# Attention and mixture-of-experts block on one core: TensorE order as written, whole mixes, a later load addition

## The chip, the cores and the metric

The kernel runs on one core of a Trainium2 chip, in one launch. Times are device microseconds from the chip's own clock; the figure for a kernel is the median of several runs. A profile is one execution of the same program with the hardware profiler on. Engines are named as in the profile: PE is TensorE (with PEld, its weight loads), DVE is VectorE, ACT is ScalarE, POOL is GpSimd, SP issues DMAs.

## What is computed

The input x is 8 sequences of 512 rows of 256 floats (fp32). Four layers follow each other, each added to x after a layer norm of its input: a scan layer, a mixture of experts, attention, and the same mixture of experts again. Cut to what matters here:

```
x = x + scan(layernorm(x))
x = x + ffn(layernorm(x))
x = x + attn(layernorm(x))
x = x + ffn(layernorm(x))

attn(x):   # per sequence, 16 heads of 16
    q, k, v = x @ Wqkv.T
    s = clip(q k^T / 4, -10, 10), masked causally
    return softmax(s) v @ Wout.T

ffn(x):    # 4096 rows, 16 experts, 4 picked per row
    picks, gains = route(sigmoid(x @ router.T))
    routed = sum of gain * (silu(x g_e) * (x u_e)) d_e over the picks
    return routed + (silu(x sg) * (x su)) sd     # shared experts
```

## The kernel before

**Stages.** There are four, one after the other: a stretch for the scan layer with the routing and the shared experts of the first mixture; the routed experts of the first mixture; a stretch for attention with the routing and the shared experts of the second mixture; the routed experts of the second mixture, with the sums that make the output. Routed and shared results go to two DRAM arrays (`parts`), and the next stage loads both and adds them (`load_sum`, L135 to L142).

**Attention, batch by batch.** `Attention.main(b)` works on one sequence, as four groups of four heads (two values of `o`, two of `w`). Because of causality, the key tiles of a group are packed into three banks (`BANKS`): key tile 0 (512 columns), tiles 3 and 1 (128 + 384), tile 2 (256). For each bank, `weights` issues one block of score matmuls (L1026, 32x128 array tiles, four heads beside each other), two exponentials on ScalarE (L1037), and on VectorE a mask with a clamp (L1040) and, for the rest, a clamp (L1048). The scores have two PSUM pairs of banks (kind `pair`), so the next block needs both exponentials of the block before the last to be done. `mix` multiplies a bank's weights by v (L1061, 128x32 tiles) into one accumulator of the group, `po`. `share` copies `po` (ScalarE), transposes it (four transposes, L1077, `pto`), and VectorE divides by the row sum (`rec`, `o_a`, L1079 and L1080). After the four groups, `o` is transposed (`pt_oa`) and projected (L416, `py_a`).

**What else stands in a batch of the stretch.** `stretch` (the function that drives both stretches) puts beside each other, in batch b: attention of b; the sends of batch b − 2 (16 indirect DMAs that GpSimd issues, L647, each after slots and gain of its rows, L630 and L637); the projections q, k, v of b + 1 (L971, L989); the shared experts of b − 2 (`pg`, L892; `pd`, L920); the norm and the logits of b − 1 for the router (`sorted_m`, L400; transposes `pt_m` and copies `xT_m`, L364 and L366; logits `pl_m`, L540); the rest of the routing; and for batch b + 2 the load, its addition (L141) and its norm (`normed`: statistics on VectorE, L378 and L379, the power `rstd_l` on GpSimd, L397, then `xn` on VectorE, L400) and transposes. Transposes, logits, projections, shared experts and `po` share four PSUM banks of kind `one`.

**What sets the order.** Each piece is a generator whose steps yield a number of columns, and `beside` always takes the piece that has done the smallest share of its columns; `timed` places steps at given shares of a batch. That is the written order. The framework's scheduler may then move an instruction on its engine ahead of others that it does not depend on, by its own estimate of when inputs are ready; so the order that each engine runs is not the written one. `tc.keep_in_program_order(made)` pins one instruction: it stays behind the instruction of its engine that was written just before it. Nothing was pinned before. Engines run their own lists in order, and wait where an input is not there.

In the old attention steps, a bank of the last group's mix follows each score block of the next group:

```
for i in range(len(BANKS)):
    yield weights(o, w, i, at)
    if last is not None:
        yield mix(*last[0:2], i, last[2])
```

**Early batches.** `prepared(b)` loads, adds and norms batches 0 and 1 of the attention stretch during the routed experts of the first mixture, by GpSimd's queue. In these experts, per block: `up` copies of weights on VectorE (L786), matmuls with `gate` and `up` (L804), and the down projection (L832).

Of the kernel before, what the change touches and what calls it, by code (L numbers as in the profile page):

```python
# [15 lines left out]
P = 128  # L16
# [54 lines left out]
def tile_hybrid_block(  # L71
# [64 lines left out]
    def load_sum(i: int, b: int, more, queue=nc.sync):  # L136

        x_sb = xpool.tile([P, NT, D], FP, tag="x", name=f"x{i}_{b}")
        queue.dma_start(out=x_sb, in_=rows_of(parts[i][0], b))
        queue.dma_start(out=more, in_=rows_of(parts[i][1], b))  # L140
        nc.vector.tensor_add(x_sb, x_sb, more)  # L141
        x_tiles[b] = x_sb  # L142


# [151 lines left out]

    class Piece:
# [53 lines left out]
    def turned(src, tag: str, into, copies, home=None):  # L353

        rows = src()
        if home is None:
            dst = work.tile([P, KD, T], FP, tag="kb4", name=f"xT_{tag}", bufs=KB)
        else:
            dst = home(f"xT_{tag}")
        into(dst)  # L360
        for k in range(KD):
            pt = bank([P, NT, P], f"pt_{tag}_{k}")
            for t in range(NT):
                nc.tensor.transpose(pt[:, t, :], rows[:, t, k * P : (k + 1) * P], ident)  # L364
            flat = pt.rearrange("p t q -> p (t q)")
            copies[k](dst[:, k, :], flat)  # L366
            yield T // 2
# [40 lines left out]
    def add_projection(b: int, lhs_of, w_sb, n: int, tag: str):  # L408

        x_sb = x_tiles[b]  # L410
        for half in range(2):
            py = bank([P, 2, D], f"py_{tag}_{half}")
            for j in range(2):
                t = 2 * half + j
                for c in range(n):
                    nc.tensor.matmul(  # L416
                        py[:, j, :],
                        lhsT=lhs_of(c)[:, t * P : (t + 1) * P],
                        rhs=w_sb[:, c, :],
                        start=(c == 0),  # L420
                        stop=(c == n - 1),
                    )
                yield n * D
            rows = x_sb[:, 2 * half : 2 * half + 2, :]
            nc.vector.tensor_add(rows, py, rows)


    class Scan:
# [21 lines left out]
        def main(self, b: int, xnT):  # L450
            tag = f"s{b}"

            def steps():
                y_sb = []
                for c in range(NI):
                    pz = bank([P, T], f"pz_{tag}_{c}")
                    for k in range(KD):
                        nc.tensor.matmul(
                            pz,
# [3 lines left out]
                            stop=(k == KD - 1),  # L463
                        )
                    bias = b_in_sb[:, c : c + 1]
# [69 lines left out]
    def logits(i: int, b: int, tag: str, held):  # L535
        xnT = held["xnT"]
        pl = bank([P, NT, E], f"pl_{tag}")
        for t in range(NT):
            for k in range(KD):
                nc.tensor.matmul(  # L540
                    pl[:, t, :],
# [3 lines left out]
                    stop=(k == KD - 1),  # L545
                )
            yield
# [4 lines left out]
    def choices(i: int, b: int, tag: str, held):  # L552
# [52 lines left out]
        flat = sel.rearrange("p t e -> p (t e)")  # L605
        nc.tensor.matmul(pr[:, 0].rearrange("p t e -> p (t e)"), lhsT=tri, rhs=flat, start=True, stop=True)
        nc.tensor.matmul(pr[:, 1].rearrange("p t e -> p (t e)"), lhsT=ones, rhs=flat, start=True, stop=True)
        row = small.tile([P, NT + 1, E], FP, tag="row", name=f"row_{tag}", bufs=3)
# [52 lines left out]
    def blocks(i: int, table):  # L661
# [60 lines left out]
        for c in range(CAND):  # L722
            nc.tensor.matmul(
                pe, lhsT=cand_e.to_broadcast([P, P]), rhs=chosen[:, c, :], start=(c == 0), stop=(c == CAND - 1)
            )
        expert = small.tile([P, NBLK], FP, tag="expert", name=f"expert_{tag}", bufs=1)
        nc.scalar.copy(expert, pe)
        lines = work.tile([1, 2, NBLK], I32, tag="col", name=f"lines_{tag}", bufs=COLS)
        for which in range(2):
            pl = bank([1, NBLK], f"pl_{tag}_{which}")  # L730
            for c in range(CAND):
                nc.tensor.matmul(
                    pl, lhsT=cand_at[:, which, c : c + 1], rhs=chosen[:, c, :], start=(c == 0), stop=(c == CAND - 1)
                )
            if which == 0:
# [11 lines left out]
    def routed(i: int, table, beside):  # L747
# [41 lines left out]
        def turn(n: int):  # L789
            rows = held[n][2]  # L790
            pt = bank([P, KD, P], f"pt_{i}_{n}", "misc")
            for k in range(KD):
                nc.tensor.transpose(pt[:, k, :], rows[:, k * P : (k + 1) * P], ident)  # L793
            nc.scalar.copy(rows[:, ROW : ROW + D], pt.rearrange("p k q -> p (k q)"))  # L794

        def up(n: int):
# [4 lines left out]
            for s in range(2):  # L801
                for f in range(KF):
                    for k in range(KD):
                        nc.tensor.matmul(  # L804
                            ph[:, s, f * P : (f + 1) * P],
# [3 lines left out]
                            stop=(k == KD - 1),  # L809
                        )  # L810
            act = rows[:, ROW + D : ROW + D + F]
# [16 lines left out]
        def down(n: int):  # L828
            w, _, rows, act, gain = held.pop(n)
            py = bank([P, D], f"pyr_{i}_{n}", "y")  # L830
            for f in range(KF):
                nc.tensor.matmul(  # L832
                    py,
# [3 lines left out]
                    stop=(f == KF - 1),  # L837
                )

# [37 lines left out]
    def shared_experts(i: int, b: int, xnT_of, tanh: bool):  # L877
# [3 lines left out]
        def steps():  # L881
            xnT = xnT_of()
            acts = []
            for n in range(NSH):
# [3 lines left out]
                for f in range(KF):  # L888
                    pair = [bank([P, T], f"pg_{tag}_{n}_{f}_{which}") for which in range(2)]
                    for dst, w in zip(pair, (g_sb, u_sb)):  # L890
                        for k in range(KD):
                            nc.tensor.matmul(  # L892
                                dst,
# [3 lines left out]
                                stop=(k == KD - 1),  # L897
                            )
                        if dst is pair[0]:
# [14 lines left out]
            for half in range(2):  # L914
                py = bank([P, 2, D], f"pd_{tag}_{half}")
                for j in range(2):
                    t = 2 * half + j
                    for n in range(NSH):
                        for f in range(KF):
                            nc.tensor.matmul(  # L920
                                py[:, j, :],
# [3 lines left out]
                                stop=(n == NSH - 1 and f == KF - 1),  # L925
                            )
                    yield NSH * KF * D
# [17 lines left out]
    class Attention:  # L945
# [7 lines left out]
        def load(self, b: int):  # L953
            load_sum(0, b, kb4(f"more0_{b}"))

        def project(self, b: int, xnT):
# [8 lines left out]
            def steps():  # L965
                nc.gpsimd.memset(v_sb, 1.0)
                for o in range(NO):
                    for which in range(2):
                        pq = bank([P, T], f"pq_{tag}_{o}_{which}")
                        for k in range(KD):  # L970
                            nc.tensor.matmul(  # L971
                                pq,
# [3 lines left out]
                                stop=(k == KD - 1),  # L976
                            )
                        if which == 0:
# [5 lines left out]
                for h in range(2):  # L984
                    pv = bank([P, 2, D], f"pv_{tag}_{h}")
                    for j in range(2):
                        t = 2 * h + j
                        for k in range(KD):
                            nc.tensor.matmul(  # L989
                                pv[:, j, :],  # L990
# [3 lines left out]
                                stop=(k == KD - 1),  # L994
                            )
                        nc.scalar.copy(
# [7 lines left out]
        def main(self, b: int, made):  # L1004
# [4 lines left out]
            def weights(o: int, w: int, i: int, at):  # L1009
# [12 lines left out]
                for c in tiles:  # L1022
                    n = T - c * P
                    for j in range(HG):
                        r = slice(32 * j, 32 * j + 32)
                        nc.tensor.matmul(  # L1026
                            ps[j // 2][:, j % 2, col : col + n],
# [3 lines left out]
                            stop=True,  # L1031
                        )
                        at[c, j] = es[j // 2][:, j % 2, col : col + n]
                    col += n
                mixed = len(tiles) * P
                for two in range(2):
# [11 lines left out]
                    nc.vector.tensor_scalar(es[two][:, :, mixed:], es[two][:, :, mixed:], LOW, TOP, ALU.max, ALU.min)  # L1048
                return T + (len(tiles) - 1) * T

            order = [c for tiles, _ in BANKS for c in tiles]

            def mix(o: int, w: int, i: int, at):
# [4 lines left out]
                for c in BANKS[i][0]:  # L1058
                    for j in range(HG):
                        h = 8 * o + 2 * j + w  # L1060
                        nc.tensor.matmul(  # L1061
                            at["po"][32 * j : 32 * j + 32, c * P : T],
# [4 lines left out]
                            tile_position=(0, 32 * j),  # L1067
                        )
                return len(BANKS[i][0]) * T

            def share(o: int, w: int, at):
# [4 lines left out]
                for t in range(NT):  # L1076
                    nc.tensor.transpose(pt[:, t].rearrange("p j c -> p (j c)"), oT[:, t * P : (t + 1) * P], ident)  # L1077
                rec = small.tile([P, NT, HG], FP, tag="rec", name=f"rec_{tag}_{o}_{w}")
# [7 lines left out]
            def steps():  # L1086
                held["o"] = kb4(f"o_{tag}")
                groups = [(o, w, {}) for o in range(NO) for w in range(2)]
                last = None
                for o, w, at in groups:  # L1090
                    for i in range(len(BANKS)):
                        yield weights(o, w, i, at)
                        if last is not None:
                            yield mix(*last[0:2], i, last[2])
                    if last is not None:
                        share(*last)
                        yield T // 2
                    last = o, w, at
                for i in range(len(BANKS)):
                    yield mix(*last[0:2], i, last[2])  # L1100
                share(*last)
                yield T // 2
                yield from turned(lambda: held["o"], f"o{tag}", lambda oT: held.update(oT=oT), by_both)
                yield from add_projection(b, lambda c: held["oT"][:, c, :], wo_sb, KD, tag)

            each = 2 * NT * T + T // 2
            return Piece(2 * NO * each + KD * T // 2 + NT * KD * D, steps())


    ready = {}  # L1110

    def prepared(b: int):
# [16 lines left out]
        def begin():  # L1129
            load_sum(0, b, free_home("v", f"more_{b}"), nc.gpsimd)  # L1130
            steps.append(normed(b, f"l1_{b}", place))
# [24 lines left out]
    def stretch(layer):  # L1156
# [39 lines left out]
        for b in range(B):  # L1196
# [25 lines left out]
            if nxt < B:  # L1222
                layer.load(nxt)
                pieces += [
# [34 lines left out]
    with banks_of(big=4, misc=2, y=2):  # L1259
        instead["one"] = "misc"  # L1260
        routed(0, table, {**prepared(0), **prepared(1)})
        del instead["one"]

    with banks_of(one=4, pair=2):
        table = stretch(Attention())

    with banks_of(big=4, misc=2, y=2):
# [78 lines left out]
```

## Time and profile before

| | |
|---|---|
| median of 6 runs | 1787.66 us (1784.38 to 1790.66) |
| profiled execution | 1785.94 us |
| its span | 1784.0 us |
| mean granted TensorE clock | 0.976 |
| attention stretch, first score block to the expert table's matmuls | 782.56 to 1324.35, 541.8 us |
| batch 0, batch 1 of it | 49.20 us, 50.00 us |
| batches 2 to 5 | 277.4 us |
| batch 6, batch 7 with what stands behind it | 67.82 us, 97.34 us |

Batches of the attention stretch are cut at the first score block of each. A profile line of a group names the source line, engine, operation, output and input, shapes and count; a bracket at the end gives the idle time of the engine just before it and what ended it. In the windows view a row is one stretch of time with the busy time and the number of instructions of PE, PEld, DVE, ACT and POOL, then the granted clock, the share of the DMA engines and GB/s.

### The profile page before, as it was taken

How to read it: one execution, taken by the hardware profiler on the slowest of the kernel's cores; microseconds unless marked ns; L12 is line 12 of the kernel's file. 1: busy time of each engine (PE TensorE's matmuls, PEld its weight loads, DVE VectorE, ACT ScalarE, POOL GpSimd, SP SyncE). 2: the span in 40 equal slices, each digit the busy share in tenths (PEclk: the TensorE clock that was granted, in tenths of full speed). 3: DMA queues.
4: the chain of work that ended last, by engine and by line, in shares of the span. 5: the costliest groups of instructions: out<-in, count | busy, mean ns of one | idle time of the engine just before them, and what ended most of it. 6: DMA issues, size and time to landing. Idle time of an engine off the chain costs nothing. (4 is left out here: it accounts for less than half of the span.)

```text
span 1784.0 us, 32535 instructions
## 1 busy us (share of the span) xinstructions
PE 1674.6 (94%) x10640; PEld 1255.1 (70%) x10640; DVE 1078.2 (60%) x3354; ACT 795.7 (45%) x1628; POOL 768.8 (43%) x667
## 2 busy tenths in 40 slices
PE   5899999989999999989999999999998999999991
PEld 3566666579998999944545545544557999999991
DVE  5878777445555555556776676566643555555552
ACT  2322222145555555545654454464414555555550
POOL 3255555535555555530042231331533555555552
PEclk9899999989999999999999999999998999999995
DMA  4443423445555655521011111121534555665557
GB/s 158 158 153 137 138 97 113 146 102 96 96 95 107 102 94 97 100 58 36 25 56 64 65 63 58 46 93 62 189 115 100 98 94 98 116 103 94 98 101 245
DMA packets 149995, 181.35 MB, mean 102 GB/s; under 512 B 16096, under 2 KB 136960, under 8 KB 149824
## 3 DMA queue, kind: packets, MB, share of 16 engines
q0 software_dynamic: 53136, 76.81, 23.1%
q1 hardware_dynamic: 94320, 96.12, 17.9%
q10 hardware_dynamic: 2368, 6.29, 0.9%
q8 instruction: 89, 1.46, 0.3%
q14 instruction: 82, 0.67, 0.1%
HBM read 81.62 MB, written 97.53 MB: 100 GB/s over the span
## 5 line engine op out<-in xcount | busy, mean ns | idle before, releaser
L841 POOL DMA_INDIRECT part<-rows x272 | 425.6, 1565 | 362.9 <-ACT rows L840 322.4
L647 POOL DMA_INDIRECT xg<-sorted_m,slots_m x256 | 260.2, 1017 | 221.6 <-DVE sorted_m L637 109.9
L804 PEld LDWEIGHTS ph<-rows,gate 128*128 128x128 f32 x2176 | 286.7, 193 | 15.7 <-ACT rows L794 1.3
L804 PE MATMUL ph<-rows,up 128*128 128x128 f32 x2176 | 289.4, 276 | 6.3 <-DVE up L786 6.3
L804 PE MATMUL ph<-rows,gate 128*128 128x128 f32 x2176 | 290.6, 277 | 0.6 <-ACT rows L794 0.6
L832 PE MATMUL pyr<-w_all,rows 128*128 x1088 | 281.4, 381 | 3.4 <-DVE rows L814 3.4
L804 PEld LDWEIGHTS ph<-rows,up 128*128 128x128 f32 x2176 | 266.7, 193 | 7.0 <-DVE up L786 7.0
L812 ACT ACTIVATE rows<-ph 128x256 f32<-128x256 f32 x272 | 104.5, 384 | 340.1 <-PE ph L804 337.4
L813 DVE TENSOR_TENSOR rows<-ph,rows 128x256 f32<-128x256 f32 x272 | 115.4, 424 | 204.0 <-ACT rows L812 204.0
L832 PEld LDWEIGHTS pyr<-w_all,rows 128*128 128x128 f32 x1088 | 185.5, 191 | 18.5 <-DVE rows L814 3.9
L786 ACT COPY gate<-w_all 128x512 f32 x272 | 170.5, 627 | 11.1 <-DVE rows L813 1.2
L1037 ACT ACTIVATE w_all<-ps_a 128x1024 f32<-128x1024 f32 x128 | 124.3, 1021 | 81.8 <-PE ps_a L1026 72.4
L840 ACT ACTIVATE rows<-pyr,gain 128x256 f32<-128x256 f32 x272 | 128.7, 473 | 18.1 <-PE pyr L832 17.4
L786 DVE COPY up<-w_all 128x512 f32 x272 | 117.8, 433 | 25.2 <-PE ph L804 23.4
L817 DVE SCALAR_TENSOR_TENSOR gain<-rows,expert_b 128x4 f32<-128x4 f32 x272 | 59.9, 221 | 117.8 <-ACT rows L840 82.5
L1026 PE MATMUL ps_a<-w_all 32*128 32x512 f32 (+3 forms) x1024 | 119.6, 468 | 7.2 <-ACT w_all L1037 5.9
L793 PE MATMUL pt<-ident,rows 128*128 128x128 f32 x544 | 105.0, 275 | 21.4 <-DMA rows<-xg 21.4
L892 PE MATMUL pg_m<-xT_m,su_sb 128*128 128x512 f32 x256 | 125.1, 611 | 0.0
L892 PE MATMUL pg_m<-xT_m,sg_sb 128*128 128x512 f32 x256 | 123.2, 604 | 0.0
L920 PE MATMUL pd_m<-sd_sb,act_m 128*128 128x256 f32 x512 | 121.1, 382 | 0.0
L814 DVE TENSOR_TENSOR rows<-ph,rows 128x256 f32<-128x256 f32 x272 | 115.2, 424 | 8.2
L920 PEld LDWEIGHTS pd_m<-sd_sb,act_m 128*128 128x128 f32 x512 | 95.5, 190 | 21.1 <-issue 3.7
(200 smaller groups left out, 2168.3 us busy)
## 6 DMA issues: line engine op xcount, KB each, us to landing
rows<-xg SPq DMA_DIRECT2D x272, 136.0 KB, 2.5
part<-x SPq DMA_DIRECT2D x16, 512.0 KB, 2.8
part<-ys_m SPq DMA_DIRECT2D x16, 512.0 KB, 2.8
w_all<-in_L_ffn_gate_w_dram SPq DMA_DIRECT2D x24, 256.0 KB, 5.0
w_all<-in_L_ffn_up_w_dram SPq DMA_DIRECT2D x24, 256.0 KB, 5.5
w_all<-in_L_ffn_down_w_dram SPq DMA_DIRECT2D x24, 256.0 KB, 5.4
xg<-zeros SPq DMA_DIRECT2D x34, 136.0 KB, 1.8
part<-rows POOLq DMA_INDIRECT x272, 4.0
```

What stands on the lines that cost most here:

```text
L647: nc.gpsimd.indirect_dma_start(out=xg[i], out_offset=bass.IndirectOffsetOnAxis(ap=slots[:, at : at + 1], axis=0), in_=rows[:, t, :], in_of ...
L786: copy(here, w_all[:, bass.ds(held[n][0] + half * KD * F, KD * F)])
L804: nc.tensor.matmul(ph[:, s, f * P : (f + 1) * P], lhsT=both[s][:, k * F + f * P : k * F + (f + 1) * P], rhs=rows[:, ROW + k * P : ROW + (k ...
L813: nc.vector.tensor_mul(act, ph[:, 0, :], act)
L814: nc.vector.tensor_mul(act, ph[:, 1, :], act)
L832: nc.tensor.matmul(py, lhsT=act[:, f * P : (f + 1) * P], rhs=w_all[:, bass.ds(w + 2 * KD * F + f * D, D)], start=(f == 0), stop=(f == KF - 1),
L840: nc.scalar.mul(rows[:, 0:D], py, gain[:, TK : TK + 1])
L841: nc.gpsimd.indirect_dma_start(out=parts[i][n % 2], out_offset=bass.IndirectOffsetOnAxis(ap=rows[:, D + 2 * TK : D + 2 * TK + 1].bitcast(U ...
L892: nc.tensor.matmul(dst, lhsT=w[:, k, f * P : (f + 1) * P], rhs=xnT[:, k, :], start=(k == 0), stop=(k == KD - 1),)
L920: nc.tensor.matmul(py[:, j, :], lhsT=acts[n][:, f, t * P : (t + 1) * P], rhs=shared[n][3][:, f, :], start=(n == 0 and f == 0), stop=(n == ...
L1026: nc.tensor.matmul(ps[j // 2][:, j % 2, col : col + n], lhsT=k_sb[w][r, o, c * P : (c + 1) * P], rhs=q_sb[r, o, c * P : T], start=True, st ...
L1037: nc.scalar.activation(es[two], ps[two][:, :, 0:cols], AF.Exp, scale=ATT_SCALE)
```

## The change

Three things are changed.

1. While the list `strict` is not empty, which is during the whole attention stretch, every TensorE instruction is pinned to written order (`ordered`).
2. In attention's steps, from batch 2 on, the mix of a group is issued whole (three banks, one after the other) right behind the next group's first score block, and its `share` behind that. In batches 0 and 1 (`apart`) a bank's mix follows each score block, as before. The columns that steps yield are given anew, and the transposes of `o` are issued at once.
3. `load_sum` issues the load of the second part ahead of the first, and its addition is a generator of two halves of 128x512, each pinned on VectorE behind what was written before it. In the attention stretch the halves are placed at 0.24 and 0.28 of the batch; in `prepared` they are issued at once.

```
 def load_sum(i: int, b: int, more, queue=nc.sync):
     x_sb = xpool.tile([P, NT, D], FP, tag="x", name=f"x{i}_{b}")
+    queue.dma_start(out=more, in_=rows_of(parts[i][1], b))
     queue.dma_start(out=x_sb, in_=rows_of(parts[i][0], b))
-    queue.dma_start(out=more, in_=rows_of(parts[i][1], b))
-    nc.vector.tensor_add(x_sb, x_sb, more)
     x_tiles[b] = x_sb
+    def added():
+        for t in range(0, NT, 2):
+            rows = x_sb[:, t : t + 2, :]
+            tc.keep_in_program_order(nc.vector.tensor_add(rows, rows, more[:, t : t + 2, :]))
+            yield
+    return added()
...
+    strict = []
+    def ordered(made):
+        if strict:
+            tc.keep_in_program_order(made)
...
-                        nc.tensor.matmul(
+                        ordered(nc.tensor.matmul(
...
             def steps():
                 held["o"] = kb4(f"o_{tag}")
                 groups = [(o, w, {}) for o in range(NO) for w in range(2)]
+                apart = b < 2
+                def mixed(last, *banks):
+                    for i in banks if last is not None else ():
+                        mix(*last[0:2], i, last[2])
                 last = None
-                for o, w, at in groups:
-                    for i in range(len(BANKS)):
-                        yield weights(o, w, i, at)
-                        if last is not None:
-                            yield mix(*last[0:2], i, last[2])
-                    if last is not None:
-                        share(*last)
-                        yield T // 2
-                    last = o, w, at
-                for i in range(len(BANKS)):
-                    yield mix(*last[0:2], i, last[2])
+                for group in groups:
+                    weights(*group[0:2], 0, group[2])
+                    mixed(last, *([0] if apart else range(len(BANKS))))
+                    yield 9 * P
+                    if last is not None and not apart:
+                        share(*last)
+                    yield 2 * P
+                    weights(*group[0:2], 1, group[2])
+                    mixed(last, *([1] if apart else []))
+                    yield 12 * P
+                    weights(*group[0:2], 2, group[2])
+                    mixed(last, *([2] if apart else []))
+                    yield 9 * P
+                    if last is not None and apart:
+                        share(*last)
+                    last = group
+                mixed(last, *range(len(BANKS)))
+                yield 9 * P
                 share(*last)
-                yield T // 2
-                yield from turned(lambda: held["o"], f"o{tag}", lambda oT: held.update(oT=oT), by_both)
+                yield 10 * P
+                issue(Piece(0, turned(lambda: held["o"], f"o{tag}", lambda oT: held.update(oT=oT), by_both)))
+                yield 9 * P
                 yield from add_projection(b, lambda c: held["oT"][:, c, :], wo_sb, KD, tag)
-            each = 2 * NT * T + T // 2
-            return Piece(2 * NO * each + KD * T // 2 + NT * KD * D, steps())
+            return Piece((2 * NO * 32 + 28) * P + NT * KD * D, steps())
...
         def begin():
-            load_sum(0, b, free_home("v", f"more_{b}"), nc.gpsimd)
+            for _ in load_sum(0, b, free_home("v", f"more_{b}"), nc.gpsimd):
+                pass
...
             if nxt < B:
-                layer.load(nxt)
+                added = layer.load(nxt)
+                if added is not None:
+                    pieces.append(timed(added, 0.24, 0.28))
                 pieces += [
                     timed(norm(nxt), *spread(0.32, 0.44, NT), *spread(0.56, 0.64, NT)),
                     timed(turn(nxt), 0.75, 0.79),
                 ]
...
+    strict.append(True)
     with banks_of(one=4, pair=2):
         table = stretch(Attention())
+    strict.clear()
```

Every TensorE call that the attention stretch reaches is wrapped by `ordered` in the same way; only one is shown.

## The prediction

> **What bounds the kernel now.** I read the busy shares first, then the attention stretch in windows of one batch each, then the timelines of TensorE, GpSimd and VectorE inside one batch. The page's own totals:
>
> ```profile
> PE 1674.6 (94%) x10640; PEld 1255.1 (70%) x10640; DVE 1078.2 (60%) x3354; ACT 795.7 (45%) x1628; POOL 768.8 (43%) x667
> ```
>
> The windows (stretch, length, then busy time of PE, PEld, DVE, ACT, POOL, the clock, the DMA share, GB/s) are cut at the first score block of batches 2, 3, 6 and 7:
>
> ```profile
> 881.76:951.48 69.72, 69.03 (x431) 35.34 (x430) 46.64 (x147) 33.78 (x48) 20.59 (x20) 1.00 0.16 56
> 951.48:1020.65 69.17, 69.08 (x429) 35.34 (x429) 46.25 (x144) 33.78 (x48) 19.83 (x20) 1.00 0.18 63
> ...
> 1159.19:1227.01 67.82, 67.74 (x421) 34.67 (x420) 41.71 (x129) 33.19 (x47) 17.72 (x18) 1.00 0.21 73
> 1227.01:1324.35 97.34, 95.65 (x516) 50.84 (x515) 69.94 (x241) 37.20 (x52) 34.86 (x37) 1.00 0.42 142
> ```
>
> In batches 2 to 7 TensorE has no gap to speak of, at full clock: its own order and shapes set the time there, and any wait it is given shows in full. Batches 2 to 5 average (1159.19 − 881.76) / 4 = 69.36 us. Batches 0 and 1 (49.20 and 50.00) have gaps of 3.2 and 2.0. Inside batch 3, two other engines matter:
>
> ```profile
> 970.38 1.01 POOL L397 TENSOR_TENSOR rstd_l<-rstd_l,neg_half 128x4 f32<-128x4 f32 x1 [15.70 <-DVE den_m L635]
> 971.57 1.06 POOL L647 DMA_INDIRECT xg<-sorted_m,slots_m  x1 [0.18 <-issue]
> ...
> 991.18 1.52 POOL L647 DMA_INDIRECT xg<-sorted_m,slots_m  x1 [0.30 <-issue]
> ```
>
> ```profile
> 960.68 1.23 DVE L141 TENSOR_TENSOR x<-x,more 128x1024 f32<-128x1024 f32 x1 [3.18 <-DMA x<-part]
> ...
> 982.98 1.38 DVE L400 TENSOR_SCALAR xn<-x,mv_l,rstd_l 128x256 f32<-128x256 f32 x4
> 985.08 0.69 DVE L366 COPY xT_m<-pt_m 128x512 f32<-128x512 f32 x1 [0.73 <-PE pt_m L364]
> ```
>
> The 16 indirect sends hold GpSimd from 971.57 to 992.70, 21.1 us. The small power that finishes the next norm (rstd_l) runs just ahead of them, so VectorE's xn, 12 us later, finds it ready. Behind xn on VectorE stands the copy xT_m that the logits matmuls need.
>
> **Part 1: order and whole mixes, the gain.** Matmul prices are start to start. In this order a mix piece (L1061) that follows another is cheaper, and a whole-array block beside one is dearer:
>
> ```profile
> 946.21 1.89 PE L416 MATMUL py_a<-w_att,xT_oa 128*128 128x256 f32 x8
> 947.94 1.89 PE L920 MATMUL pd_m<-sd_sb,act_m 128*128 128x256 f32 x8
> ...
> 1211.32 1.06 PE L1061 MATMUL po_a<-w_all,v_a 128*32 128x512 f32 x8
> 1212.31 1.99 PE L920 MATMUL pd_m<-sd_sb,act_m 128*128 128x256 f32 x8
> 1214.24 1.07 PE L1061 MATMUL po_a<-w_all,v_a 128*32 128x128 f32 x16
> 1215.12 0.61 PE L1061 MATMUL po_a<-es_a,v_a 128*32 128x256 f32 x8
> ```
>
> A projection block among its like takes 947.94 − 946.21 = 1.73; between two mix pieces 1214.24 − 1212.31 = 1.93: 0.10 for each side. A mix piece followed by another takes 1215.12 − 1214.24 = 0.88 instead of 0.99. The written order has 13 whole-array visits between score and mix blocks in a steady batch instead of 22: 9 × 0.20 = 1.8. Two pieces of each of four mixes are followed by mix: 8 × 0.11 = 0.9. And the scheduler's split score blocks vanish: the 512 block split 2 and 6 costs 1.05 (942.94 to 943.99) + 1.07 (951.48 to 952.55) against 1.07 whole, so 1.05; the 256 block split in halves costs 2 × 0.63 (968.58 to 969.22, 970.28 to 970.91) against 0.64, so 0.6. Sum 4.35 a batch: priced this way a steady batch falls from 68.15 to 63.8, the last-but-one from 67.04 to 63.0, the last (to the table) from 94.55 to 90.1.
>
> [...]
>
> **Part 2: waits that written order brings.** A block that finds its input late now stops TensorE; before, another was pulled in front. A whole mix stands right after the next group's 512 score block, but needs the previous group's last weights, for which ScalarE's exponentials (1.02 each, two a block) and VectorE's masks come late: stepping the first group of batch 3 through the new orders with these durations gives 2.7, and 0.5 for small things elsewhere. Bounds: 0, if VectorE runs ahead, and 4 × 2.7 = 10.8, if every group waits so; I take 2.7 + 0.5 = 3.2, since later groups have 2 to 4 whole-array blocks between and the first has none.
>
> [...]
>
> **Part 3: the moved addition, and the power behind the sends.** One 128x1024 add (1.23) becomes two 128x512. Two halves cost about 1.3 together, all of it on VectorE, which has slack. The swap of the loads does nothing: on SP's queue the scheduler had already put `more` ahead of x from x_3 on, x_2's pair changes places at a quiet point, and x can't go before its buffer's last reader is done (+5.45 in batch 3), whatever stands ahead of it; GpSimd's two loads keep their order. In the changed VectorE order the first half is not late: it stands just behind one sorted_m, so VectorE still waits for x until +9.2 (960.68 above, idle 3.18). The second half comes after the first group's o_a. So the norm ends later, and GpSimd's order flips: in batches 2 to 5 the 16 sends now come ahead of rstd_l (before: behind). VectorE's order puts xn and the second group's reciprocal ahead of the third group's 256 masks and the second half of xT_m. Counted from the batch's start:
> - the gain row is written at +18.4 in the new order (before 970.62 − 951.48 = +19.1), the sends end at 18.5 + 21.1 = +39.6, and the power takes 0.2 + 1.0: +40.8.
> - VectorE reaches xn at about +30.7 and stands still for some 10 us; behind it wait rec and o_a (0.24 + 0.42), two masks and two clamps of 512 (0.60 + 0.34 each pair) and xT_m: 1.38 + 0.66 + 1.88 + 0.69 = 4.6, so xT_m is there at +45.4.
> - TensorE reaches the logits, 33.97 into its work, at 33.97 + 3.2 = +37.2 and can't pass them: 8.2 of idle, the largest new cost.
> - the rest, 63.8 − 33.97 = 29.8, and 0.2 of waits: a batch of 75.4, against 69.36: **+6.0**, in four batches **+24.0**. Without that wait a batch would be 67.2. Bounds for the wait: 0, and 8.2 + 3, if the masks lost behind xn are late for the third mix as well; I take 8.2, because three queue orders and one measured duration give it.
>
> **Part 4: elsewhere.** Batches 0 and 1 have no sends. They keep bank-by-bank mixes; their blocks, priced as above, fall from 88.95 to 82.6, but the windows are 49.20 + 50.00 = 99.2, so 10.3 lie above the priced blocks, in part the gaps (5.2), for exponentials, which less filler makes longer; between −6.3 (waits stay as they are) and +5 (two groups in each wait 1.25 more for exponentials) I take +0.5. Batch 6 has no next norm: 63.0 + 1.0 − 67.82 = −3.8. Batch 7: 90.1 + 4.0 − 97.34 = −3.2, with 2.8 waits before and 1.2 more taken for its whole mixes. In the routed experts before the stretch the adds are run at once, but with the pinned order the up copy stands behind the adds' stats too:
>
> ```profile
> 567.24 1.23 DVE L141 TENSOR_TENSOR x<-x,more 128x1024 f32<-128x1024 f32 x1 [6.01 <-DMA more<-part]
> 568.38 0.42 DVE L786 COPY up<-w_all 128x512 f32 x1
> 568.86 1.16 PE L804 MATMUL ph<-rows,up 128*128 128x128 f32 x8 [1.26 <-DVE up L786]
> ```
>
> TensorE is waiting for that copy; it ends 2.2 later at two places, partly absorbed: 1.3 each, 2.6 (bounds 0 and 5).
>
> Sum: 0.5 + 24.0 − 3.8 − 3.2 + 2.6 = **+20.1**. On the profiled execution, 1785.94 (1784.0 span and 1.9 around it), that is 1806.0; the median of the runs, 1787.66, lies 1.7 higher: 1807.8.
>
> **Rivals.**
> - Faster: the power behind the sends stays off TensorE's path. Batches 2 to 5 are then 67.2 each, −8.6 together, and the total 0.5 − 8.6 − 3.8 − 3.2 + 2.6 = −12.5: 1775.2. It decides when xT_m is ready by +37.2, so the power by +32.6, 8.2 earlier; the sign turns at xT_m by +40.3, 5.1 earlier. For it: the shares of VectorE (67%) and GpSimd (29%) in a batch leave slack. Against: the sends took 21.1 to 21.2 in every batch, and both queues run in order.
> - No change: the wait is about 3 instead of 8, which cancels the rest, 1784 to 1791. Nothing in the profile puts the sends 5 us earlier.
> - The addition does what it says: its late place takes the 3.2 of idle from VectorE, gain and sends come 3 earlier, four batches lose 12 less: 1796. Against: the first half's place in VectorE's order.
> - Worse: VectorE's 10 us of lost time are not regained in the 30 that follow, and each later group's mix waits 0.75 to 1.5 more, 12 to 18 in all: 1820 to 1826. VectorE has 46.25 of work in a batch of 75, which speaks against it.
>
> **How the numbers follow.** Forecast 0.55, around 1798 to 1817; the addition's rival 0.10; worse 0.16; no change 0.05; faster 0.14. The range 1784 to 1826 leaves out most of the faster case and the far end of the worse one. What the measurement can tell from no change is about 0.2%, 3.6 us: faster 0.14, within 0.04, slower 0.82. Predicted: 1807.5, range 1784 to 1826.
>
> **What would show it.** In batches 2 to 5 of the changed profile: rstd_l on GpSimd right after the last send near +40; xn on VectorE with about 10 us of idle ahead of it put down to GpSimd; the first logits matmul of a batch with 8 of idle put down to xT_m; steady batches near 75, batch 6 near 64, mix pieces in threes at 0.88, 0.88, 0.55. If the first logits wait is under 3, or steady batches are under 69, the forecast is wrong at part 3.

## The result and the profile after

The changed kernel takes 1829.66 us (median of 8 runs, 1823.92 to 1831.06) against 1785.51 us (median of 18 runs of the kernel before): the ratio is 1.0242, 95% interval 1.0229 to 1.0256. It is 44 us slower; 20 were forecast. Its profiled execution took 1825.69 us, span 1824.0, 40.0 more than the span before. By stage, cut at the same blocks of TensorE:

| stage | before | after | change | forecast |
|---|---|---|---|---|
| scan stretch, to the first expert table | 343.46 | 344.11 | +0.65 | 0 |
| first expert table to first score block | 439.10 | 445.70 | +6.6 | +2.6 |
| batches 0 and 1 | 99.20 | 104.69 | +5.5 | +0.5 |
| batches 2 to 5 | 277.43 | 312.63 | +35.2 | +24.0 |
| batch 6 | 67.82 | 65.49 | −2.3 | −3.8 |
| batch 7, to the second expert table | 97.34 | 95.57 | −1.8 | −3.2 |
| second expert table to the end | 459.65 | 455.81 | −3.8 | 0 |

The last row is no sign of an effect: another trace of the changed kernel (f0 below) has 462.8 there.

The windows of the changed kernel (stretch, length, busy time of PE, PEld, DVE, ACT and POOL, clock, DMA share, GB/s) for batches 2, 3, 6 and 7:

```profile
894.50:972.26 77.76, 68.53 (x429) 36.08 (x428) 46.70 (x146) 33.76 (x48) 19.83 (x20) 0.96 0.14 50
972.26:1050.38 78.12, 69.14 (x430) 36.41 (x429) 46.33 (x145) 33.77 (x48) 19.84 (x20) 0.93 0.16 56
...
1207.13:1272.62 65.49, 64.05 (x422) 34.31 (x421) 41.76 (x129) 33.21 (x47) 18.02 (x18) 1.00 0.22 75
1272.62:1368.19 95.57, 92.02 (x518) 51.31 (x518) 69.43 (x241) 37.32 (x52) 34.97 (x37) 1.00 0.43 144
```

Batch 3 was 69.17 long with TensorE busy for all but 0.09; now it is 78.12 long, with a gap of 9, and the clock is 0.93 where it was 1.00. Batch 6, the first without a next norm, has neither. Three timelines of batch 3 (start, length, engine, line, operation; in brackets the idle time just before and what ended it) show the gap. GpSimd first:

```profile
990.28 1.44 POOL L662 DMA_INDIRECT xg<-sorted_m,slots_m  x1 [14.85 <-DVE sorted_m L652]
...
1010.31 0.96 POOL L662 DMA_INDIRECT xg<-sorted_m,slots_m  x1 [0.30 <-issue]
1011.29 1.05 POOL L412 TENSOR_TENSOR rstd_l<-rstd_l,neg_half 128x4 f32<-128x4 f32 x1
```

```profile
1002.87 0.69 DVE L922 SCALAR_TENSOR_TENSOR act_m<-sig_m,pg_m 128x512 f32<-128x512 f32 x1 [1.27 <-PE pg_m L907]
1012.38 0.41 DVE L415 TENSOR_SCALAR xn<-x,mv_l,rstd_l 128x256 f32<-128x256 f32 x1 [8.83 <-POOL rstd_l L412]
...
1015.97 0.69 DVE L381 COPY xT_m<-pt_m 128x512 f32<-128x512 f32 x1
```

```profile
1008.78 0.71 PE L1041 MATMUL ps_a<-w_all 32*128 32x256 f32 x8
1013.59 0.61 PE L555 MATMUL pl_m<-rw_sb,xT_m 128*128 128x16 f32 x2 [4.09 <-DVE o_a L1093]
1016.71 0.61 PE L555 MATMUL pl_m<-rw_sb,xT_m 128*128 128x16 f32 x2 [2.51 <-DVE xT_m L381]
1017.15 3.76 PE L907 MATMUL pg_m<-xT_m,sg_sb 128*128 128x512 f32 x4
1020.85 1.61 PE L1041 MATMUL ps_a<-w_all 32*128 32x512 f32 x8
1022.39 1.93 PE L1075 MATMUL po_a<-w_all,v_a 128*32 128x512 f32 x24
```

The power rstd_l stands behind the last send; VectorE waits 8.83 for it with xn at the head of its list; TensorE waits at the logits, first for the PSUM bank that o_a frees (4.09), then for xT_m (2.51). And there is a cost that the prediction did not have: the next pg block takes 1020.85 − 1017.15 = 3.70 instead of 1.82 to 1.91, and the score block after it 1.54 instead of 1.07. The clock in windows there, and at three other places behind waits:

```profile
572.39:578.10 5.71, 5.71 (x22) 5.35 (x23) 4.35 (x19) 1.75 (x4) 4.35 (x4) 0.50 0.63 106
...
776.15:784.75 8.60, 8.60 (x16) 3.76 (x17) 0.75 (x1) 1.86 (x3) 1.76 (x2) 0.81 0.58 145
796.36:803.80 7.44, 7.44 (x20) 2.54 (x20) 3.87 (x9) 2.75 (x4) 0.00 (x0) 0.54 0.01 2
...
1017.15:1022.39 5.24, 5.24 (x14) 1.68 (x14) 1.86 (x6) 0.00 (x0) 0.00 (x0) 0.55 0.00 0
1022.39:1028.30 5.91, 5.91 (x56) 3.30 (x52) 3.31 (x11) 4.52 (x6) 0.00 (x0) 1.00 0.00 0
```

Behind the stall the mean clock is 0.55 for 5.24 us, at 0.50 from 1017.15 to 1021.50, and then 1.00 again.

### The profile page after: what moved, and what is told of

It reads as the page before. It is cut to its first block, busy times and chain, and to the rows that moved or that the text cites. A ratio compares the mean times of both kernels' runs of the same rounds, so it can differ in the third digit from the quotient of the medians.

```text
span 1824.0 us, 32551 instructions
## 1 busy us (share of the span) xinstructions
PE 1671.1 (92%) x10640; PEld 1263.5 (69%) x10640; DVE 1082.7 (59%) x3362; ACT 795.4 (44%) x1628; POOL 767.8 (42%) x667
## 5 line engine op out<-in xcount | busy, mean ns | idle before, releaser
L907 PE MATMUL pg_m<-xT_m,sg_sb 128*128 128x512 f32 x256 | 132.2, 641 | 0.0
L1041 PE MATMUL ps_a<-w_all 32*128 32x512 f32 (+3 forms) x1024 | 110.2, 481 | 12.2 <-ACT w_all L1052 10.0
L809 ACT COPY rows<-pt 128x256 f32<-128x256 f32 x272 | 99.8, 368 | 20.0 <-PE pt L808 19.7
```

The costliest lines, as they stand in the source:

```text
L907: ordered(nc.tensor.matmul(dst, lhsT=w[:, k, f * P : (f + 1) * P], rhs=xnT[:, k, :], start=(k == 0), stop=(k == KD - 1),))
```

## The experiments

Theory A: the power behind the sends stalls VectorE and so TensorE, and the stall takes the clock with it. Theory B: written order and whole mixes cost by themselves. Others came up on the way. In all tables "steady" is the length of one of batches 2 to 5, "start" the time from the first expert table to the first score block.

**Four kernels on another chip.** Edits: the power on VectorE (e1), the old load and addition in the changed kernel (e2), no pins on TensorE (e3), and the kernel before with the new load and addition alone (e4).

```
e1: -    return normed(b, f"l{i}_{b}", place)
    +    return normed(b, f"l{i}_{b}", place, by_vector=i == 1)
e2: load_sum and its callers as before (one add at the load)
e3: -    strict.append(True)
e4: the kernel before, with load_sum and its callers as in the change
```

> The changed kernel with one edit: in the attention stretch the power of the next norm is made on VectorE (a dozen small instructions) instead of on GpSimd. Theory A (the power queued behind the 16 sends stalls VectorE, then TensorE, and the clock falls behind the stall): the logits no longer wait, steady batches 2 to 5 fall from 78.2 to 67 to 70 us at clock 1.00, the whole to 1783 to 1797 us; the later start of the stretch (+6.6) and the longer batches 0 and 1 (+5.5) stay. Theory B (written order and whole mixes cost by themselves): steady batches stay over 75, the whole over 1820.

> The changed kernel with load and addition as before (one 128x1024 add, not pinned, issued with the load); TensorE order and whole mixes stay. As built, the power then stands ahead of the sends on GpSimd again. Theory A: no stall at the logits, steady batches 67 to 69 us, the stretch starts 0 to 1 us later than before instead of 7, the whole 1775 to 1787 us. Theory B: steady batches over 75, the whole over 1815.

> The changed kernel without the pins on TensorE; whole mixes and the moved addition stay, and so does the order on GpSimd (sends ahead of the power). Theory A: the stall stays, steady batches 76 to 79 us, the whole 1818 to 1831 us. Theory B, with the pins as what costs: steady batches near 69, the whole under 1800.

> The kernel before with part 3 of the change alone (loads swapped, two pinned halves at 0.24 and 0.28). As built, the power stays ahead of the sends on GpSimd here. Theory A: steady batches as before, 69 to 70 us, only the later start of the stretch (+6 to 7) remains, the whole 1786 to 1794 us. A rival, theory C (the later addition by itself makes VectorE late, whatever GpSimd's order): steady batches over 75, the whole over 1810.

On the chip of these four runs the kernel before took 1893.85 us, 108 more than on the others. The ratios were 1.0030 (1.0007 to 1.0052), 1.0079 (1.0051 to 1.0107), 1.0015 (0.9984 to 1.0047) and 1.0024 (1.0000 to 1.0048). ScalarE and VectorE of e2 in batch 3:

```profile
1050.51 0.59 ACT L1079 COPY oT_a<-po_a 128x512 f32<-128x512 f32 x1 [11.80 <-remote]
```

```profile
1050.51 0.69 DVE L914 SCALAR_TENSOR_TENSOR act_m<-sig_m,pg_m 128x512 f32<-128x512 f32 x1 [10.88 <-remote]
```

Both are released in the same instant by something that the trace does not name, 2.4 us after the last send ended (1048.06). In e2 it happens at every block of sends; e1, e3 and e4 have such stops too, most of them of 7 us and more, and none of the traces of the other chips has one. Such a stop covers the stall in question, so the four runs tell nothing of it; what makes it was not settled. Three of them were run again elsewhere, with the changed kernel beside them.

**Power, addition and pins, one at a time.**

> The changed kernel itself, beside the next three on one chip. Where the kernel before takes about 1786 us: 1824 to 1831, steady batches 78. In the four runs ahead of this, the kernel before took 1894, and all engines stood still for some 10 us at each block of sends; if that is so here too, theory A says that the changed kernel is within 1% of the kernel before, since its stall falls into the same stretch.

> The changed kernel with load and addition as before. Where the kernel before takes about 1786 us, theory A (the power behind the sends): steady batches 67 to 69 us, the whole 1775 to 1787. Theory B (written order and whole mixes cost by themselves): over 75 and over 1815. Where the kernel before takes about 1894: 1.005 to 1.01 of it, as in the run ahead of this.

> The changed kernel with the power on VectorE. Where the kernel before takes about 1786 us, theory A: steady batches 67 to 70 us, the whole 1783 to 1797. Theory B: over 75 and over 1820. Where the kernel before takes about 1894: 1.00 to 1.005 of it.

> The changed kernel without the pins on TensorE, the sends still ahead of the power. Where the kernel before takes about 1786 us, theory A: steady batches 76 to 79 us, the whole 1818 to 1831. Theory B with the pins as the cost: steady batches near 69, the whole under 1800. Where the kernel before takes about 1894: 1.00 to 1.005 of it.

| kernel (before: 1786.15) | us | ratio, interval | start | batches 0, 1 | steady |
|---|---|---|---|---|---|
| f0, the change | 1831.20 | 1.0240 (1.0215 to 1.0265) | 446.0 | 106.3 | 78.6 |
| f1, power on VectorE | 1793.36 | 1.0043 (1.0026 to 1.0060) | 443.1 | 105.1 | 68.7 |
| f2, old addition | 1794.73 | 1.0048 (1.0031 to 1.0065) | 441.7 | 107.8 | 69.8 |
| f3, no pins | 1822.68 | 1.0207 (1.0189 to 1.0225) | 444.3 | 100.4 | 77.5 to 78.4 |

f1 is theory A's direct test: with one argument added, the same order on TensorE loses the stall, and 9.5 us a batch come back. Its logits come without a gap, at clock 1.00 (996.64 to 1000.00):

```profile
995.99 0.71 PE L1041 MATMUL ps_a<-w_all 32*128 32x256 f32 x8
996.64 0.62 PE L555 MATMUL pl_m<-rw_sb,xT_m 128*128 128x16 f32 x4
```

f3 shows that pins are no cause of the stall. f1 lies inside the ranges that theory A gave; f2 lies over both of its own (67 to 69 and 1775 to 1787). And without the stall little is gained: 68.7 is hardly below the 69.4 of before, and 69.8 is above it. The first reason is in f1's mix behind the second group's first score block, the others further on in the same batch:

```profile
971.11 1.27 PE L1075 MATMUL po_a<-w_all,v_a 128*32 128x512 f32 x12
972.67 1.18 PE L1075 MATMUL po_a<-w_all,v_a 128*32 128x128 f32 x12 [0.29 <-DVE w_all L1055]
974.05 0.63 PE L1075 MATMUL po_a<-es_a,v_a 128*32 128x256 f32 x4 [0.19 <-DVE es_a L1063]
975.25 0.63 PE L1075 MATMUL po_a<-es_a,v_a 128*32 128x256 f32 x4 [0.58 <-DVE es_a L1063]
975.81 1.13 PE L1004 MATMUL pv_a<-w_att,xT_l 128*128 128x256 f32 x4
...
981.08 1.13 PE L1004 MATMUL pv_a<-w_att,xT_l 128*128 128x256 f32 x4 [0.69 <-ACT v_a L1011]
...
1009.60 0.70 PE L1041 MATMUL ps_a<-w_all 32*128 32x256 f32 x4 [0.53 <-ACT w_all L1052]
1010.52 0.70 PE L1041 MATMUL ps_a<-w_all 32*128 32x256 f32 x4 [0.21 <-ACT w_all L1052]
1011.15 1.12 PE L907 MATMUL pg_m<-xT_m,su_sb 128*128 128x512 f32 x2
```

From 971.11 to 975.81 it takes 4.70, where a whole mix that finds its input takes 988.06 − 985.77 = 2.29: 2.4 of waits for VectorE's masks. pv waits 0.7 for ScalarE, and the last group's 256 score block, in two halves, waits for exponentials: from the end of the block before it (1009.07) to 1011.15 it takes 2.08 instead of 0.64, 1.4 more. In f2, where the 1.23 us add stands in front of the masks, the first mix takes 5.73.

**What is left.** Edits to f1: no pins (g1), and the old interleaved mixes in all batches (g2); e4 again (g3); and a combination of what seemed worth keeping (g4).

```
g2: -    apart = b < 2
    +    apart = True
g4: f1, with  + if i == 1 and b == 2: strict.append(True)  as the only pins,
    and in prepared one add at once, not pinned, as before
```

> Power on VectorE and no pins on TensorE; whole mixes and the moved addition stay. Theory P (pins cost at the start of the stretch and in batches 0 and 1, where TensorE waits for ScalarE, and are worth little later): batches 0 and 1 fall from 105 to 99 to 101 us together, the stretch starts 1 to 2 us earlier, steady batches stay at 68.2 to 69.2, the whole 4 to 8 us under the run with power on VectorE and pins (1.000 to 1.002 of the kernel before). Rival (pins are what makes steady batches short): steady batches over 69.5, the whole no better than 1.004.

> Power on VectorE, pins, but a bank's mix behind each score block in all batches, as written in the kernel before. Theory: whole mixes save at TensorE's mode changes but wait for masks, some 2.4 us behind the first group and 1.4 at the last, so the two orders are close: steady batches 68 to 71 us, the whole 1.003 to 1.01. Rival (whole mixes are worth the 4.3 us a batch that the prices say): steady batches over 72, the whole over 1.012.

> The kernel before with part 3 alone, on a chip where the kernel before takes about 1786 us. The power stays ahead of the sends as built. Theory A: steady batches 69 to 70 us, only the later start of the stretch (+4 to 6) remains, 1788 to 1794 us. Theory C (the later addition makes VectorE late by itself): over 75, over 1810.

> What the runs say is worth keeping: power on VectorE; pins on TensorE from batch 2 on only; whole mixes; the moved addition in the stretch but one add as before, not pinned, in the routed experts ahead of it. Theory: the stretch starts as before (439 to 440 us behind the first table), batches 0 and 1 99 to 101 together, steady batches 68.5 to 69, the last two 162 to 163: 1776 to 1783 us, 0.995 to 0.998 of the kernel before. If the pins act on batches 0 and 1 in another way, or the later batches need the early pins, no better than 1.0.

| kernel (before: 1787.74) | us | ratio, interval | start | batches 0, 1 | steady |
|---|---|---|---|---|---|
| g1 | 1789.11 | 0.9999 (0.9984 to 1.0015) | 446.6 | 109.5 | 68.9 |
| g2 | 1778.16 | 0.9932 (0.9908 to 0.9957) | 447.5 | 106.5 | 66.0 |
| g3 | 1793.21 | 1.0034 (1.0021 to 1.0048) | 444.6 | as before | 69.0 |
| g4 | 1784.08 | 0.9978 (0.9962 to 0.9994) | 439.8 | 102.1 | 68.7 |

Theory C falls with g3: the later addition alone leaves the steady batches as they were, and costs 5.5 us ahead of the stretch. g4 has the start of before once the old add is back there, but its time lies 1 us over the 1776 to 1783 that was expected, and its batches 0 and 1 over 99 to 101. g1's start and first batches (446.6 and 109.5) were to be shorter than f1's and are longer. The windows of batches 0 and 1 show why, first g1's and then those of h2 and k1 (edits below), which differ by the pins alone:

```profile
793.42:902.93 109.51, 102.05 (x698) 48.41 (x697) 72.94 (x224) 59.12 (x82) 3.48 (x5) 0.91 0.05 15
```

```profile
788.16:894.68 106.52, 95.91 (x697) 46.76 (x697) 69.33 (x202) 59.08 (x82) 5.53 (x7) 0.95 0.05 16
```

```profile
785.82:886.24 100.42, 93.12 (x697) 45.51 (x697) 69.89 (x202) 58.92 (x82) 5.53 (x7) 1.00 0.05 17
```

Without pins TensorE idles 109.51 − 102.05 = 7.5 (g1) and 7.3 (k1), with them 10.6 (h2) and 10.3 (the change, 789.81 to 894.50): pins cost 3 us of waits there. The rest goes with the clock, 0.91 in g1, 0.95 in h2, 0.97 in the change and 1.00 in k1: g1 and k1 differ by 9.1 us in these two batches, with 7.5 and 7.3 of waits. g1's profiled execution, 1797.56, was also the longest of its runs. Its steady batches do speak to theory P: without pins 68.9. g2 contradicts both of its theories: interleaved mixes are 2.7 us a batch shorter than whole ones, outside the range of 68 to 71 from below. (The mode changes of its theory are the places where 128x32 mix tiles and whole-array blocks follow each other, which the prediction's rows price at 0.10 a side.)

**Which part turned GpSimd's order, and where the gain is.**

```
h1: g4 with apart = True          h2: the change with apart = True
h3: the kernel before, with TensorE pinned from batch 2 on
```

> The combined version with a bank's mix behind each score block in all batches: power on VectorE, pins from batch 2 on, the moved addition in the stretch, the old one ahead of it. Theory D (whole mixes cost 2.7 us a steady batch, pins save 3.4): steady batches 66 us, the stretch starts as before, 1769 to 1776 us, 0.990 to 0.994. If whole mixes were not what differed between the last runs, no better than 0.997.

> The changed kernel with one edit: a bank's mix behind each score block in all batches. As built, the power then stands ahead of the sends on GpSimd again, with the moved addition and all pins in place. Theory A with D: no stall at the logits, steady batches 66 to 67 us, the later start of the stretch and the longer batches 0 and 1 stay, the whole 1778 to 1788, 0.995 to 1.001. If the stall came from the moved addition alone: steady batches over 74, over 1810.

> The kernel before with pins on TensorE from batch 2 on alone; steps, mixes, addition and power as before. The power stays ahead of the sends as built. Theory D: pins save by themselves, steady batches 66 to 68 us against 69.2, the whole 1774 to 1784, 0.993 to 0.998. If pins only gain together with the other parts: steady batches over 69, 0.999 or more.

```
k1: h2 without strict.append(True)     k2: e2 with apart = True
k3: h1 without pins, the power on GpSimd
```

> The changed kernel with the old interleaved mixes and no pins: the columns that the steps yield and the moved addition are what is left of parts 1 to 3. Theory E (the new columns order the steady batches, the pins add little there and cost in batches 0 and 1): steady batches 65.5 to 67.5, batches 0 and 1 together 100 to 104 against 106.5 with pins. Rival (the columns gain only when they are pinned): steady batches 68 to 70.

> The changed kernel with the old mixes and the old load and addition: pins and new columns alone. Theory: without whole mixes no block waits for VectorE's masks, so the place of the addition is worth nothing: steady batches 66 to 66.5. Rival (the moved addition gains by itself, as it did by 1.1 us with whole mixes): 67 or more.

> New columns, old mixes, the moved addition in the stretch and the old one ahead of it, power on GpSimd as before, no pins at all. Theory E: the stretch starts as before, batches 0 and 1 100 to 102 together, steady batches 65.5 to 67.5: 1770 to 1778 us. Rival: steady batches 68 to 70, 1780 or more.

| kernel (before: 1787.60 for h, 1787.36 for k) | us | ratio, interval | start | batches 0, 1 | steady |
|---|---|---|---|---|---|
| h1 | 1773.26 | 0.9923 (0.9900 to 0.9945) | 439.7 | 101.9 | 66.0 |
| h2 | 1778.70 | 0.9947 (0.9926 to 0.9968) | 444.6 | 106.5 | 66.0 |
| h3 | 1786.33 | 0.9998 (0.9983 to 1.0014) | 440.4 | as before | 69.4 |
| k1 | 1771.83 | 0.9921 (0.9901 to 0.9941) | 443.1 | 100.4 | 66.1 |
| k2 | 1775.47 | 0.9930 (0.9914 to 0.9947) | 441.5 | 106.6 | 66.0 |
| k3 | 1768.56 | 0.9895 (0.9878 to 0.9911) | 439.7 | 100.7 | 66.1 |

With one line of the change undone, h2 is 51 us faster than the change and faster than the kernel before. Its batch 3 in the windows, and GpSimd in it:

```profile
960.67:1026.65 65.98, 65.52 (x430) 34.71 (x429) 46.58 (x145) 33.90 (x48) 19.69 (x20) 1.00 0.19 67
```

```profile
976.04 1.12 POOL L412 TENSOR_TENSOR rstd_l<-rstd_l,neg_half 128x4 f32<-128x4 f32 x1 [12.17 <-DVE rstd_l L411]
980.01 1.44 POOL L662 DMA_INDIRECT xg<-sorted_m,slots_m  x1 [2.85 <-DVE sorted_m L652]
```

The power is ahead of the sends again, though the addition is as late as in the change. Steady batches of the four combinations, pins and new columns in all:

| | addition moved | addition as before |
|---|---|---|
| whole mixes | 78.2 (the change) | 69.8 (f2) |
| interleaved mixes | 66.0 (h2) | 66.0 (k2) |

Only whole mixes and the moved addition together put the sends ahead of the power (in f3 too, which has both without pins); by what estimate the scheduler comes to that is not shown. h3 refutes theory D's second half (pins save nothing by themselves), and k1 confirms theory E. The new columns (and the transposes of `o` at once, which no run takes apart from them) set the written order and make the steady batch some 3 us shorter: 66.1 in k1 against 69.0 in g3, both without pins and with the moved addition, and 66.0 in k2 against 69.4 in h3, both with pins and the old addition. What changed can be counted in the timelines of a steady batch: whole-array blocks stand between score and mix blocks 22 times in the kernel before and in g3, 20 times in h3, but 13 times in h2 and k2 and 14 times in k1 and k3. k3, without pins and whole mixes and with the old add ahead of the stretch, beats both kernels: 18.8 us under the kernel before, and 1.4 under the range that was expected of it.

## Why the prediction was right and where it failed

The direction and the mechanism of the stall were right, the size was less than half, and the time lies above the range. Of the 20 us by which the profile went past the forecast, 11.2 stand in batches 2 to 5 and 9.0 ahead of them. By its steps:

- **Part 3, the wait: right, to within 1.4 us.** Forecast and measured in batch 3, counted from 972.26: sends from +18.5, measured +18.0; sends over at +39.6, measured +39.0; the power done at +40.8, measured +40.1; VectorE idle for some 10, measured 8.8; xT_m there at +45.4, measured +44.4; TensorE at the logits at +37.2, measured +37.2.
- **Part 3, "the rest, 63.8 − 33.97 = 29.8, and 0.2 of waits": this step failed.** From the second pair of logits to the next batch it is 1050.38 − 1016.71 = 33.7, 3.7 more. Behind the stall, at the mean clock of 0.55, pg takes 1.9 more and the score block 0.5 more. The last group's 256 score block, which waits for exponentials in two halves, takes 1033.47 − 1031.38 = 2.09 instead of 0.64. So a batch is 78.2 instead of 75.4, in four batches 11.2 us.
- **Part 3, why GpSimd's order flips: half of it.** It was put down to the late norm alone. g3 and h2 have the same late addition and no flip; f2 has whole mixes and no flip: it takes both.
- **Part 1, the gain of 4.35: its prices held, but one part of it was a bad bargain.** f1 has the forecast's order on TensorE without the stall; its batch less the three waits of part 2 is 68.7 − 4.5 = 64.2, and 63.8 were forecast. The nine visits and the unsplit score blocks, 1.8 + 1.05 + 0.6 = 3.45, need no whole mixes: h2 has the same 13 visits with interleaved ones and gains 69.2 − 66.0 = 3.2. The 0.9 for mix beside mix is what brings most of the waits, so that whole mixes cost 2.7 net (68.7 in f1 against 66.0 in g2).
- **Part 2, waits of 3.2 a batch: mis-sized.** The first whole mix waits 2.4, near the 2.7 that were forecast; but pv waits 0.7 and the last 256 score block 1.4, which the 0.5 for small things was to cover: 4.5 in all, and f1's batch is 68.7, not 67.2.
- **Part 4, the start of the stretch: +6.6, over its upper bound of 5.** The up copy was late at both places, as said, by more than was summed: waits of 3.79 (1.26 before) and 3.49, each with 5.7 us at clock 0.50 behind it. g3 has 5.5 of it, from the split add; pins add some 1.5 (after and f0 against f3), since the pv matmuls of batch 0 wait for ScalarE, where f3 runs the same 16 in 3.62 without a wait:

```profile
763.35 2.07 PE L819 MATMUL ph<-rows,up 128*128 128x128 f32 x8 [3.49 <-DVE up L801]
...
776.15 8.77 PE L986 MATMUL pq_a<-xT_l,w_att 128*128 128x512 f32 x16 [2.46 <-PEq L889]
...
786.29 1.99 PE L1004 MATMUL pv_a<-w_att,xT_l 128*128 128x256 f32 x8 [0.51 <-ACT v_a L1011]
788.75 1.13 PE L1004 MATMUL pv_a<-w_att,xT_l 128*128 128x256 f32 x4 [0.46 <-ACT v_a L1011]
```

- **Part 4, batches 0 and 1: +5.5, over its bound of +5.** Most of it comes with the pins: 106.5 with them (h2), 100.4 without (k1). Of these 6 us, 3 are waits, as in the windows above; the rest goes with the clock, 0.95 in h2 against 1.00 in k1, which the sum had at nothing.
- **The rivals.** The faster one named the right condition, the power off TensorE's path: where it holds, the kernel is 0.4 to 0.5% slower with whole mixes (f1, f2) and 0.5% faster with interleaved ones (h2). The range failed because none of its cases had a clock that falls behind waits, and because the costs ahead of batch 2 were bounded too low.

The profile of before held the sign of it: 3.18 us of idle ahead of the stretch, and then a projection of 16 matmuls that took 779.01 − 770.37 = 8.64, at a mean clock of 0.80:

```profile
770.37 8.80 PE L971 MATMUL pq_a<-xT_l,w_att 128*128 128x512 f32 x16 [3.18 <-PEq L874]
779.01 3.62 PE L989 MATMUL pv_a<-w_att,xT_l 128*128 128x256 f32 x16
```

In f1 the same block comes after 1.72 of idle and takes 780.58 − 773.64 = 6.94, at clock 1.00.

## What to carry to other kernels

When a scheduler orders several engines, read the built order of the engines that are not the bound: here a four-column power moved behind 21 us of indirect sends, and no line of the diff touches either. Three waits of TensorE cost more than themselves here: behind 3.49 and 3.79 us the next 5.7 us ran at clock 0.50, and behind 2.46 us a projection block took 8.60 at a mean clock of 0.81, where f1's, behind 1.72 us, took 6.94 at 1.00. So read from the trace the clock of the blocks behind a wait, and price them with it. Price a packed order with its inputs' lateness before its cheaper neighbours: a whole mix saves 0.1 us for each neighbour, and the first one waited 2.4 us for its masks; fewer visits of whole-array blocks and unsplit score blocks came with 3 us a batch less and hardly a wait.

## What the runs showed of the hardware

- **Clock.** Blocks behind a gap on TensorE of 1.72 us (f1) ran at clock 1.00; behind 2.46 the window's clock was 0.81; behind 3.49 and 3.79 it was 0.50 for 5.7 us. In these runs the length of the last gap alone does not decide it: in batch 0 the changed kernel, behind gaps of 0.53, 0.42 and 0.91, ran at 0.54 (796.36 to 803.80), and the kernel before, behind 0.54, 0.42 and 0.91, ran at 1.00 (789.11 to 797.35). What does decide it was not shown.
- **One chip that stops at sends.** On one chip the kernel before took 1893.85 us instead of 1786, and in the four traces taken there ScalarE, VectorE and behind them TensorE stopped during the blocks of 16 indirect sends: in e2 ScalarE for 11.80 us and VectorE for 10.88 at the block of batch 3; in e1 ScalarE for 13.94 to 15.70 at six blocks of the scan stretch and for 7.58 to 11.35 at six of the attention stretch, with TensorE behind the latter idle for 5.32 to 9.38. What holds them is not in the trace.
